# Layer 3 of a graph attention network: totals from pairs of blocks added on DVE, and a row of R anew for each chunk

## The chip, the cores and the metric

The kernel runs on one core of one Trainium2 chip. The metric is the device time of one execution in microseconds. Before the change it is 2934.87 us, the median of three runs (2932.88 to 2935.89). The engines of the core are TensorE (PE), VectorE (DVE), ScalarE (ACT), GpSimd (POOL) and SyncE (SP); each works through its own queue of instructions in order, and they wait for each other by semaphores.

## What is computed

Sixteen graphs of 1024 nodes with 256 features go through four attention layers, each with layer norm and ReLU ahead of it and a residual sum behind it. Layer 3, which the change touches, has four heads of 64 features:

```python
h = einsum('bnd,hde->bhne', nodes_embed, W)          # 4 heads of 64
for t in range(n_types):
    weight += (node_adj == t + 1) * (e_src[:, :, t, :, None] + e_dst[:, :, t, None, :])
weight = where(node_adj == 0, NEG, leaky_relu(weight, 0.01))
dst = einsum('bhij,bhje->bhie', softmax(weight), h) + bias
out = relu(dst) + h
out = (out - mean(out)) / sqrt(var(out) + EPS) * ln_gamma + ln_beta     # by head
x = x + out
```

The adjacency holds 0 and 1 only, so one edge type counts. The kernel writes the exponential of a leaky sum as a product of factors of the two nodes times the larger of two terms. One term is a row over all targets (R), the other a column of the source block. A softmax is then a sum of values times weights, divided by the sum of weights (the totals).

## The kernel before

The 16 batches go in two streams, even and odd ones. Each stream is a Python generator that yields an estimate of time; a loop takes the next piece of the stream that is behind, and the second stream starts `LAG` = 111 units late. So one stream's layer 3 lies beside the other stream's layers 0 to 2. The framework's scheduler then orders the instructions of each queue, within what the waits and `keep_in_program_order` allow.

A layer of attention (layers 0 to 2, `attend`) makes one row of R (`weigh`, a PSUM tile of two banks of which there is only one), eight weight tiles of 128 x 1024 from it on DVE (L367), and then eight accumulators of eight matmuls each (L461), of which two are in PSUM per stream. Each accumulator is evicted over DVE (L385, L386), ScalarE (L393, L395) and DVE (L396, L397), or on DVE alone in layer 0 (L501). Then the next layer's projection follows by pairs of blocks (`project`: L302 on DVE, transposes L338, ScalarE's copy L340, matmuls L345, evictions L413 and L417).

Layer 3 does for each of four heads: a row of R (the first by transposes, L374; the others from thirds of the factors in bf16, L574), eight weight tiles on DVE (L367), 64-wide values (`add_values`) and totals (`add_totals`) on TensorE. Both use tiles of 32 columns, four matmuls side by side (`in_tiles`, L586). The totals use the factor q of each source (column E of V3) as the stationary side, for each of eight blocks and two halves: 16 matmuls a head, beside 32 for the values. `acc` and `total` are both held in PSUM until the head's end, ScalarE copies them (L663), transposes turn them (L670, L678), DVE divides (L681) into `y`, and `center` and `rescale` normalise on DVE, ACT and POOL into `y`, which is then written to HBM (L704). A head's weight tiles are made while the head before is in its products, eight at a time, from one row of R; all of it comes in steps of four source blocks (`for first in range(0, NI, 4)`), here called chunks.

Of the kernel before, what the change touches and what calls it, by code (L numbers as in the profile page):

```python
# [32 lines left out]
F32 = mybir.dt.float32  # L33
BF = mybir.dt.bfloat16
# [7 lines left out]
P = 128  # L42
# [19 lines left out]
def short_path(ctx: ExitStack, tc: tile.TileContext, ins: dict, out: bass.AP, bad: bass.AP):  # L62
# [8 lines left out]
    NH = N // HALF  # L71
    NG = HALF // P
    EXT = [3, 3, 3, 3 * H]
    LAG = 111.0
    QUAD = P // 4
    ROOT_D = D**0.5
    ROOT_E = E**0.5
# [273 lines left out]

    row_taken = []

    def weigh(b: int, turn, c, op, into: list):

        while row_taken:
            yield 0.25
        row_taken.append(b)  # L360
        r = psum.tile([P, N], F32, name="row", bufs=1)
        for i in range(NI):
            turn(r[:, ts(i, P)], i)
        yield 0.5
        for j in range(NI):
            w = edges.tile([P, N], F32, name=f"weights{b % 2}")
            nc.vector.scalar_tensor_tensor(w, r, c(j), masks[b][:, j // 2, :, j % 2], op0=op, op1=ALU.mult)  # L367
            into.append(w)
            if j == NI - 1:
                row_taken.pop()  # L370
            yield 0.5

# [28 lines left out]
    def batch(b: int):  # L401
# [130 lines left out]


        h3, ex = last["h3"], last["ex"]
        y = single.tile([P, NI, H, E], F32, name="y")
        normed = []

        def center(h: int, blocks=slice(0, NI), engine=nc.gpsimd):
# [27 lines left out]
        def weigh3(h: int):  # L566
            if h == H:
                return iter(())
# [7 lines left out]
            return weigh(  # L576
                b, from_thirds if h > 0 else along_row(lambda i: ex[:, i, 2 * H : 2 * H + 1]),
                lambda j: ex[:, j, H + h : H + h + 1], ALU.max, weights,
            )

        def in_tiles(parts, accT: bass.AP, first: bool, last: bool):
# [11 lines left out]
        def halves_of(h: int, j: int):  # L593
            return [weights[h * NI + j][:, ts(g, HALF)] for g in range(NH)]
# [19 lines left out]
        behind = weigh3(0)  # L614
        yield from start(behind, b)
# [8 lines left out]
        for h in range(H):  # L624


            acc = accumulator(b)
            total = accumulator(b)
            if h == 0:
                for first in range(0, NI, 4):  # L630
                    for _ in range(4):
                        next(behind)
                    pinned = []
                    for j in (first + 2, first):
                        add_values(h, j)
                    yield 3.6
                for _ in behind:
                    pass
                turned_thirds = psum.tile([3 * QUAD, P], BF, name="misc")
                made = nc.tensor.transpose(  # L640
                    turned_thirds, thirds.rearrange("p t i h -> p (t i h)"), ident_bf
                )
                tc.keep_in_program_order(made)
                thirds_T = small.tile([3 * QUAD, P], BF, name="thirds_T", bufs=1)
                nc.scalar.copy(thirds_T, turned_thirds)
            behind = weigh3(h + 1)
            yield from start(behind, b)

            for first in range(0, NI, 4):
                pinned = []  # L650
                for j in (first + 2, first):
                    add_totals(h, j)
                    if h > 0:
                        add_values(h, j)
                for _ in range(4):
                    next(behind, None)
                yield 1.8 if h == 0 else 5.4
            for _ in behind:
                pass
            copies = []  # L660
            for accT in (acc, total) if h == 0 else (total, acc):
                copies.append(wide.tile([P, HALF], F32, name="sums"))
                nc.scalar.copy(copies[-1], accT)  # L663
                next(testing)
                next(coming, None)
            sums, totals = copies if h == 0 else copies[::-1]
# [20 lines left out]
            if h > 0:  # L687
                rescale(*normed.pop())


            if b < B - 1:
                normed.append(center(h))
            elif h < H - 1:
                normed.append(center(h, engine=nc.gpsimd if h < H - 2 else nc.vector))
            else:
                normed += [center(h, slice(g * NG, g * NG + NG), nc.vector) for g in range(NH)]
            yield 1.0
        for _ in coming:
# [406 lines left out]
```

## Time and profile before

| | us | share of the span |
|---|---|---|
| median of the runs | 2934.87 | |
| the profiled execution | 2933.13 | |
| its span, first to last instruction | 2931.4 | |
| attention matmuls (L461), TensorE busy | 1435.6 | 49% |
| values and totals of layer 3 (L586) | 691.7 | 24% |
| weight tiles of layer 3 (L367 from `ex`), DVE busy | 629.0 | 21% |
| weight tiles of layers 0 to 2 (L367 from `V`) | 473.7 | 16% |
| rows of R from thirds (L574), TensorE busy | 29.7 | 1% |

An fp32 matmul appears as two records. Records of matmuls overlap, so a group's busy time is more than what it adds to the end; the spacing from start to start tells the latter. The lines of the trace read `start, length, engine, line, operation, out<-in, count`, with the idle time ahead of the group in brackets and what ended it. A row of stages reads `stretch, length`, then the busy times of PE, weight load, DVE, ACT and POOL with their counts, the granted TensorE clock, the DMA share and GB/s.

### The profile page before, as it was taken

To read this page: it belongs to the slowest core of one execution; us is meant where nothing else is said; L and a number is where in the kernel's file an instruction comes from. 1 tells how busy PE (TensorE), PEld (TensorE's weight loads), DVE (VectorE), ACT (ScalarE), POOL (GpSimd) and SP (SyncE) were. 2 spreads that over 40 slices of the span, in tenths; PEclk is the share of its full clock that TensorE was granted. 3 is DMA by queue.
4 is the path that set the end of the run, shared out by engine and by line. 5 is a ranking of instruction groups with operands and counts; after the bars stand their busy time and mean duration, and the time that the engine had idled before them with its cause. 6 is when DMAs were issued, how large, how long until landed. Compare 5 with 4: busy or idle time off the path is not lost.

```text
span 2931.4 us, 44756 instructions
## 1 busy us (share of the span) xinstructions
PE 2810.0 (96%) x16790; PEld 1961.9 (67%) x16790; DVE 2147.9 (73%) x4490; ACT 1088.2 (37%) x3010; POOL 981.3 (33%) x1533
## 2 busy tenths in 40 slices
PE   7999999999999999999999999999999999999986
PEld 5775857668576685766758577685766857667552
DVE  5658688586976859778586885868768587685857
ACT  1333434343343433424334343433434334343332
POOL 2123324243242423424233242432424224242333
PEclk9999999999999999999999999999999999999998
DMA  8204022030321303122031220303203031110101
GB/s 126 39 8 65 30 30 58 8 51 29 37 51 16 56 17 51 37 29 59 1 51 37 30 58 8 51 30 37 51 12 47 29 49 39 15 30 1 22 22 31
DMA packets 127967, 106.14 MB, mean 36 GB/s; under 512 B 79872, under 2 KB 98432, under 8 KB 127744
## 3 DMA queue, kind: packets, MB, share of 16 engines
q0 software_dynamic: 47328, 66.10, 15.4%
q1 hardware_dynamic: 79568, 35.53, 5.4%
q8 instruction: 135, 2.21, 0.3%
q10 hardware_dynamic: 848, 1.57, 0.2%
q14 instruction: 88, 0.72, 0.1%
HBM read 153.49 MB, written 33.55 MB: 64 GB/s over the span
## 4 chain that ended last, share of the span: by engine, by line
PE 59%; DVE 26%; issue 8%; POOL 3%; ACT 3%; DMA 0%; POOLq 0%; ACTq 0%; SPq 0%; DVEq 0%
PE acc L461 36%; DVE weights L367 16%; PE acc L586 10%; PE acc L345 9%; PE misc L338 2%; DVE centered L302 2%; POOL rstd L293 2%; DVE V L417 1%; PE row L374 1%; POOL y L544 1%; DVE y L545 1%; DVE var L555 1%; ACT square L309 1%; DVE y L551 1%; DVE mean L549 1%
## 5 line engine op out<-in xcount | busy, mean ns | idle before, releaser
L461 PE MATMUL acc<-V,weights 128*128 128x257 f32 x6144 | 1435.6, 384 | 33.5 <-DVE weights L367 15.7
L461 PEld LDWEIGHTS acc<-V,weights 128*128 128x128 f32 x6144 | 1136.6, 190 | 281.9 <-DVE weights L367 75.3
L586 PE MATMUL acc<-weights,V 128*32 128x512 f32 x6144 | 691.7, 596 | 12.0 <-DVE weights L367 8.1
L367 DVE SCALAR_TENSOR_TENSOR weights<-row,ex,mask 128x1024 f32<-128x1024 f32 x512 | 629.0, 1272 | 97.3 <-PE row L574 65.8
L345 PE MATMUL acc<-W,hT 128*128 128x259 f32 (+1 forms) x2048 | 516.1, 389 | 38.1 <-ACT hT L340 26.9
L367 DVE SCALAR_TENSOR_TENSOR weights<-row,V,mask 128x1024 f32<-128x1024 f32 x384 | 473.7, 1273 | 0.8 <-PE row L374 0.8
L345 PEld LDWEIGHTS acc<-W,hT 128*128 128x128 f32 x2048 | 378.7, 190 | 135.1 <-ACT hT L340 44.4
L586 PEld LDWEIGHTS acc<-weights,V 128*32 128x32 f32 x6144 | 189.1, 110 | 417.7 <-issue 410.3
L393 ACT ACTIVATE below<-acc,inv 128x256 f32<-128x256 f32 x256 | 121.1, 473 | 813.1 <-DVE inv L386 569.6
L293 POOL TENSOR_TENSOR rstd<-rstd,minus_half 128x2 f32<-128x2 f32 (+1 forms) x321 | 292.8, 912 | 20.3
L309 ACT ACTIVATE square<-x_b,minus_mean 128x256 bf16<-128x256 f32 x504 | 255.7, 507 | 110.3 <-DVE minus_mean L332 105.3
L441 POOL TENSOR_TENSOR x_b<-x_b,beta 128x256 f32<-128x256 f32 x128 | 93.5, 731 | 488.6 <-ACT square L309 483.5
L292 POOL TENSOR_SCALAR rstd<-squared 128x2 f32<-128x2 f32 x252 | 80.0, 317 | 464.0 <-ACT square L309 451.0
L385 DVE TENSOR_SCALAR inv<-acc 128x1 f32<-128x1 f32 x256 | 39.1, 153 | 255.3 <-PE acc L461 254.0
L302 DVE TENSOR_SCALAR centered<-x_b,minus_mean 128x256 f32<-128x256 f32 x504 | 195.7, 416 | 5.1
L340 ACT ACTIVATE hT<-misc 128x512 f32<-128x512 f32 x256 | 150.2, 592 | 129.6 <-PE misc L338 129.3
L396 DVE SCALAR_TENSOR_TENSOR x_b<-below,x_b 128x256 f32<-128x256 f32 x256 | 131.8, 515 | 84.9 <-ACT below L393 83.0
L663 ACT COPY sums<-acc 128x512 f32<-128x512 f32 x128 | 74.9, 585 | 308.6 <-PE acc L586 301.0
L413 ACT ACTIVATE V<-acc,rstd 128x3 f32<-128x3 f32 x384 | 98.4, 261 | 231.1 <-PE acc L345 230.6
L417 DVE TENSOR_SCALAR V<-acc,rstd,V 128x256 f32<-128x256 f32 x256 | 131.4, 537 | 59.8 <-ACT V L413 58.9
L338 PE MATMUL misc<-ident,centered 128*128 128x128 f32 x1024 | 158.7, 277 | 13.7 <-DVE centered L325 11.5
L170 POOL DMA_DIRECT2D adj_i<-in_adj_dram x128 | 74.4, 582 | 290.1 <-ACT adj_i L175 248.8
(96 smaller groups left out, 2212.8 us busy)
## 6 DMA issues: line engine op xcount, KB each, us to landing
adj_i<-in_adj_dram POOLq DMA_DIRECT2D x128, 256.0 KB, 3.9
x_b<-in_x_dram SPq DMA_DIRECT2D x15, 1024.0 KB, 6.4
narrow<-in_adj_dram POOLq DMA_DIRECT2D x60, 256.0 KB, 9.3
out_dram<-y POOLq DMA_DIRECT2D x30, 512.0 KB, 7.5
x_b<-in_x_dram ACTq DMA_DIRECT2D x4, 256.0 KB, 6.1
narrow_half<-in_adj_dram POOLq DMA_DIRECT2D x4, 256.0 KB, 16.9
mask<-narrow SPq DMA_TRANSPOSE x60, 3.7
weights<-in_L_gnn_a_dram SPq DMA_DIRECT2D x3, 256.0 KB, 5.5
```

The source lines that it names most:

```text
L293: nc.gpsimd.tensor_tensor(r, r, minus_half.to_broadcast([P, n]), op=ALU.pow)
L302: nc.vector.tensor_scalar(centered[:, n, :], xb[:, 2 * pair + n, :], minus_mean[:, n : n + 1], 0.0, op0=ALU.add, op1=ALU.max,)
L309: nc.scalar.activation(square, xb[:, 2 * pair + n, :], AF.Square, bias=minus_mean[:, n : n + 1], accum_out=squared[:, n : n + 1],)
L338: nc.tensor.transpose(turned[:, k, ts(n, P)], centered[:, n, ts(k, P)], ident)
L340: nc.scalar.mul(hT, turned, ROOT_D)
L345: nc.tensor.matmul(projected, hT[:, k, ts(n, P)], W[l][:, k, :], start=(k == 0), stop=(k == NK - 1),)
L367: nc.vector.scalar_tensor_tensor(w, r, c(j), masks[b][:, j // 2, :, j % 2], op0=op, op1=ALU.mult)
L393: nc.scalar.activation(below, acc[:, :D], AF.Exp, scale=inv)
L396: nc.vector.scalar_tensor_tensor(xi, below, 1.0, xi, op0=ALU.min, op1=ALU.add)
L417: nc.vector.tensor_scalar(V[:, i, :D], projected[:, :D], rstd, V[:, i, D : D + 1], op0=ALU.mult, op1=ALU.mult,)
L461: nc.tensor.matmul(accs[i], weights[j][:, ts(i, P)], V[:, j, : D + 1], start=(j == 0), stop=(j == NI - 1),)
L586: made = nc.tensor.matmul(accT[ts(n, QUAD), :], values, moving, start=first, stop=last)
```

## The change

- The totals are no longer taken from the eight weight tiles. `add_up` adds two source blocks on DVE, the first times a ratio of the two blocks' q, in one `scalar_tensor_tensor`; the totals then need half of the matmuls. The sums go to two buffers `added`. The ratio is made once a batch by a reciprocal and a product.
- A row of R is made for each chunk of four source blocks of heads 2 to 4 (`weigh` with `blocks`), so the one PSUM tile is held for four weight tiles instead of eight. The first head's row still serves eight.
- The work of a head is spread: each chunk now yields more steps to the other stream, a head's totals are added one chunk later, and its `close` (copy, transposes, division, normalisation) runs inside the next head's first chunk. `total` is a PSUM tile taken at the second chunk. `LAG` is 112.
- `y` is no buffer of its own any more but the value part of V3; the last addition of `rescale` writes into `xb`, and the output is written from there.

```diff
-    LAG = 111.0
+    LAG = 112.0
...
-    def weigh(b: int, turn, c, op, into: list):
+    def weigh(b: int, turn, c, op, into: list, blocks=range(NI)):
...
-        for j in range(NI):
+        for j in blocks:
...
-            if j == NI - 1:
+            if j == blocks[-1]:
...
-        y = single.tile([P, NI, H, E], F32, name="y")
+        y = V3[:, :, :, :E]
...
-            engine.tensor_add(yh, yh, xb[:, blocks, head])
+            engine.tensor_add(xb[:, blocks, head], yh, xb[:, blocks, head])
...
-        def add_totals(h: int, j: int):
+        added, totals_of = {}, {}
+
+        def add_totals(h: int, first: int):
             parts = [
-                (V3[:, j + n, h, E:].to_broadcast([P, QUAD]), halves_of(h, j + n)[g])
-                for g, n in ((0, 1), (0, 0), (1, 1), (1, 0))
+                (
+                    V3[:, first + 2 * n + 1, h, E:].to_broadcast([P, QUAD]),
+                    added[h, first, n][:, ts(g, HALF)],
+                )
+                for g in range(NH)
+                for n in range(2)
             ]
-            in_tiles(parts, total, j == 2, j == NI - 4)
+            in_tiles(parts, totals_of[h], first == 0, first > 0)
+
+        def add_up(h: int, first: int):
+            for n in range(2):
+                s = added[h, first, n] = single.tile([P, N], F32, name="added", bufs=2)
+                j = first + 2 * n
+                w, w1 = weights[h * NI + j], weights[h * NI + j + 1]
+                nc.vector.scalar_tensor_tensor(
+                    s, w, ratio[:, j + 1, h : h + 1], w1, op0=ALU.mult, op1=ALU.add
+                )
...
+        behind = weigh3(0)
+        yield from start(behind, b)
+        for _ in behind:
+            yield 0.5
+        ratio = ex[:, :, :H]
+        nc.vector.reciprocal(ratio, ratio)
+        nc.gpsimd.tensor_mul(ratio[:, 1:], ratio[:, 1:], V3[:, : NI - 1, :, E])
+        closing = iter(())
+        to_add = []
+        for h in range(H):
+            acc = accumulator(b)
+            for first in range(0, NI, 4):
+                pinned = []
+                for j in (first + 2, first):
+                    add_values(h, j)
+                if first > 0:
+                    totals_of[h] = accumulator(b)
+                if to_add:
+                    add_totals(*to_add.pop())
+                if first == 0 and h > 0:
+                    closing = close(*to_close)
+                add_up(h, first)
+                to_add.append((h, first))
+                yield 2.5
+                if h == 0 and first == 0:
...
+                if h < H - 1:
+                    yield from weigh3(h + 1, range(first, first + 4))
+                yield 2.0
+                yield from closing
+                closing = iter(())
+                yield 2.0
+            sums = copy_of(acc)
+            to_close = h, sums
+        pinned = []
+        add_totals(*to_add.pop())
+        yield from close(*to_close)
...
-                y[:, ts(g, NG)].rearrange("p (c t) h e -> p c t (h e)", t=2),
+                xb[:, ts(g, NG), :].rearrange("p (c t) f -> p c t f", t=2),
```

More of the change, by code (lines that the diff above doesn't have):

```diff
@@ L561, in rescale, with weigh3 @@
             engine.tensor_mul(yh, yh, gamma[:, head].unsqueeze(1).to_broadcast(shape))
-            engine.tensor_add(yh, yh, xb[:, blocks, head])
+            engine.tensor_add(xb[:, blocks, head], yh, xb[:, blocks, head])
         weights = []
-        def weigh3(h: int):
-            if h == H:
-                return iter(())
+        def weigh3(h: int, blocks=range(NI)):
             def from_thirds(r: bass.AP, i: int):
@@ L577, in weigh3 @@
                 b, from_thirds if h > 0 else along_row(lambda i: ex[:, i, 2 * H : 2 * H + 1]),
-                lambda j: ex[:, j, H + h : H + h + 1], ALU.max, weights,
+                lambda j: ex[:, j, H + h : H + h + 1], ALU.max, weights, blocks,
             )
@@ L604, in add_values @@
                 in_tiles(parts, acc, n == 3, n == NI - 4)
-        def add_totals(h: int, j: int):
+        added, totals_of = {}, {}
+        def add_totals(h: int, first: int):
             parts = [
-                (V3[:, j + n, h, E:].to_broadcast([P, QUAD]), halves_of(h, j + n)[g])
-                for g, n in ((0, 1), (0, 0), (1, 1), (1, 0))
-            ]
-            in_tiles(parts, total, j == 2, j == NI - 4)
-        behind = weigh3(0)
-        yield from start(behind, b)
+                (
[4 more added lines that the diff above has]
+                for n in range(2)
+            ]
+            in_tiles(parts, totals_of[h], first == 0, first > 0)
[7 more added lines that the diff above has]
+                )
         rest = small.tile([P, NI, H], F32, name="rest", bufs=1)
@@ L623, in batch, with copy_of, close @@
         nc.gpsimd.tensor_sub(thirds[:, 2], rest, thirds[:, 1])
[L624 to L666, printed above, removed]
+        def copy_of(accT: bass.AP) -> bass.AP:
+            copied = wide.tile([P, HALF], F32, name="sums")
+            nc.scalar.copy(copied, accT)
+            next(testing)
+            next(coming, None)
+            return copied
+        def close(h: int, sums: bass.AP):
+            totals = copy_of(totals_of.pop(h))
             yield 0.5
@@ L686, in batch @@
             yield 0.5
-            if h > 0:
+            if normed:
                 rescale(*normed.pop())
@@ L695, in batch @@
             else:
-                normed += [center(h, slice(g * NG, g * NG + NG), nc.vector) for g in range(NH)]
+                normed.extend(
+                    center(h, slice(g * NG, g * NG + NG), nc.vector) for g in range(NH)
+                )
             yield 1.0
+        behind = weigh3(0)
[23 more added lines that the diff above has]
+                if h == 0 and first == 0:
+                    turned_thirds = psum.tile([3 * QUAD, P], BF, name="misc")
+                    made = nc.tensor.transpose(
+                        turned_thirds, thirds.rearrange("p t i h -> p (t i h)"), ident_bf
+                    )
+                    tc.keep_in_program_order(made)
+                    thirds_T = small.tile([3 * QUAD, P], BF, name="thirds_T", bufs=1)
+                    nc.scalar.copy(thirds_T, turned_thirds)
+                if h < H - 1:
[9 more added lines that the diff above has]
+        yield from close(*to_close)
         for _ in coming:
```

## The prediction

> **What bounds the kernel now.** I read the page's busy shares, its chain and its costliest groups first. TensorE is busy 96% of the span and leads the chain; DVE has 27% to spare.
>
> ```profile
> PE 2810.0 (96%) x16790; PEld 1961.9 (67%) x16790; DVE 2147.9 (73%) x4490; ACT 1088.2 (37%) x3010; POOL 981.3 (33%) x1533
> ...
> PE 59%; DVE 26%; issue 8%; POOL 3%; ACT 3%; DMA 0%; POOLq 0%; ACTq 0%; SPq 0%; DVEq 0%
> ...
> L586 PE MATMUL acc<-weights,V 128*32 128x512 f32 x6144 | 691.7, 596 | 12.0 <-DVE weights L367 8.1
> ```
>
> Then I cut one batch period out of the middle: from one first row of R (L374 from `ex`) at 1446.75 to the next at 1625.24, 178.5 us, with a cut wherever TensorE writes a row of R. The columns are stretch, length, then busy time of PE, weight load and DVE.
>
> ```profile
> 1446.75:1462.82 16.07, 15.81 (x119) 8.31 (x117) 11.75 (x17) 3.11 (x10) 3.35 (x10) 1.00 0.01 2
> 1462.82:1473.78 10.96, 10.96 (x97) 5.07 (x93) 10.30 (x10) 4.35 (x9) 1.17 (x2) 1.00 0.32 49
> 1473.78:1488.63 14.85, 14.15 (x93) 8.13 (x90) 14.25 (x21) 4.01 (x7) 5.99 (x8) 1.00 0.26 37
> 1488.63:1503.08 14.45, 13.95 (x97) 8.81 (x96) 14.17 (x29) 4.00 (x12) 4.56 (x6) 1.00 0.78 73
> 1503.08:1543.28 40.20, 40.02 (x275) 24.72 (x273) 30.55 (x70) 19.47 (x50) 15.94 (x18) 1.00 0.31 53
> 1543.28:1568.87 25.59, 23.30 (x114) 18.78 (x113) 22.77 (x46) 13.17 (x44) 14.06 (x18) 1.00 0.25 83
> 1568.87:1625.24 56.37, 56.31 (x273) 48.67 (x272) 29.15 (x88) 20.05 (x60) 16.38 (x35) 1.00 0.00 1
> ```
>
> The average hides two regimes. Where heads of layer 3 run (lines 2 to 4), DVE is busy 94 to 98%; in the last line it is half idle. Matmuls overlap in the records, so I price them by the spacing of starts in TensorE's timeline: 16 of L461 in 3.47 us, 48 of L586 in 5.29, 16 of L345 in 3.56, four transposes in 0.44. The period's work is then 169.7 us, and 8.8 are lost, most of it (3.7) in line 6, where projections wait for each other's evictions; lines 2 to 5 lose 0.4, 1.75, 0.85 and 1.2.
>
> At the start of layer 3, TensorE has other work while DVE makes the first four weight tiles:
>
> ```profile
> 1446.75 1.04 PE L374 MATMUL row<-ident,ex 128*128 128x128 f32 x8
> 1447.62 0.60 PE L338 MATMUL misc<-ident,centered 128*128 128x128 f32 x4
> 1448.06 3.63 PE L461 MATMUL acc<-V,weights 128*128 128x257 f32 x16
> 1451.53 1.04 PE L345 MATMUL acc<-W,hT 128*128 128x259 f32 x4
> 1452.83 3.64 PE L586 MATMUL acc<-weights,V 128*32 128x512 f32 x32 [0.26 <-DVE inverses L385]
> ```
>
> ```profile
> 1447.82 4.86 DVE L367 SCALAR_TENSOR_TENSOR weights<-row,ex,mask 128x1024 f32<-128x1024 f32 x4 [1.79 <-PE row L374]
> ```
>
> The fillers take 4.9 us, the four tiles 4.86: the wait is 0.26 us. What happens without such cover is seen at the end, where the last batch is alone:
>
> ```profile
> 2853.03 9.89 PE L586 MATMUL acc<-weights,V 128*32 128x512 f32 x64 [5.04 <-DVE weights L367]
> ```
>
> ```profile
> 2853.00:2855.00 2.00, 1.97 (x12) 0.50 0.00 0
> ```
>
> 5.04 us of waiting, and after it a granted clock of 0.50.
>
> [...] L396 (two SBUF inputs) has a median of 424 ns, but 1.51 us at 1521.34, beside a POOL operation from 1521.31 to 1522.58. [...] L545 with 512 keeps 0.60 us of spacing[...].
>
> **The change, part by part.** Sums are against this execution's 2931.4 us; the runs' median of 2934.9 lies 3.5 higher.
>
> Removed: each head's totals take 8 instructions in place of 16. An fp32 one is two records, so 8 x 2 x 4 heads x 16 batches = 1,024 records; 48 follow each other in 5.29 us, 110 ns each: -112.9 us of TensorE. Totals alone (16 at 1463.81, followed at 1465.67) cost the same.
>
> Added on TensorE: heads 2 to 4 write R twice. 3 x 8 x 16 = 384 records, eight in 0.45 us: +21.5. Net -91.
>
> Added on DVE: `add_up`, 4 per head, 256 operations on two SBUF tiles. [...] from above 1.27 (the recorded L367); I take 1.16: +297 us, and DVE goes from 73% to some 84%. [...] POOL is busy 33%, DMA issues aside about 0.29; that times a residual of 0.45 us is 0.13 each, 33 us. [...] half reaches TensorE: +16 (0 to 33).
>
> Moved: I cut the built order of both kernels at the rows of R and put the same spacings on it (on DVE: weights 1.19, 512 elements 0.62, evictions 0.33 to 0.48). Before, each batch repeats the seven lines above. After, two unlike batches make a period, because layer 3 now reaches over more of the other stream: 327.4 us of TensorE against 339.4 for two batches before, and 302 of DVE against 256. DVE's slack is nearly all in one stretch (63 of TensorE, 30 of DVE); in the other 264 us of TensorE, DVE has 272. So the engines are level there, and each wait between them counts.
>
> *Even batches from the third on, start of layer 3.* Behind the row from `ex` only four projection instructions (1.8 us) are left as filler: the 16 attention records have gone elsewhere. Walked by hand from the end of that row (0): DVE makes three weight tiles, two evictions (L417) and the fourth tile by 5.7; TensorE, idle since 1.8, waits 4.0 for it. The first values end at 9.3. The next transposes wait 1.5 for `centered`, which stands on DVE behind tiles five to eight (10.5). The other values and the totals end at 15.7. DVE has made two sums by 13.4, but the next two need the two `added` buffers, which these totals free: so they start at 15.7, and with two evictions and the four tiles of head 2, which stand behind them, DVE is at 23.9. TensorE is ready at 18.5 for the other stream's row of R; that needs the one PSUM tile of rows, which those four tiles read: 5.4 us of waiting. Behind that row in TensorE's queue stand head 2's values and the other stream's attention. With 0.6 for the copy of thirds_T the stretch loses 11.5, against 0.7 before.
>
> The first even batch still has fillers; for the other seven that is 7 x 10.8 = +76. Waits of 4 and 5 us can halve the clock, as above. There, L586's first 24 records at 0.50 took 4 us in place of 2.6, about 1.5 too much: seven times +10 (0 to 20).
>
> *The later heads.* Here a head's weights are made two chunks ahead, and the walk finds slack: 2.2 us of waiting in an even batch, where before lost 3.8 in lines 3 to 5. In an odd one it finds 5.7, of which 2.0 is an accumulator of the other stream: its reciprocal stands behind a sum on DVE, ScalarE's eviction behind that, and the next attention product waits for the bank. Over two batches 7.9 against 7.6: nothing. The loss of line 6 I leave as it is.
>
> *The tail.* Alone, the last layer 3 is DVE's: 16 more sums are 18.6, of which DVE's 7.9 idle us at 2857.6 takes a part: +10.
>
> At nothing: `y` in V3, the final add into `xb` and the output from `xb` (same shapes and queues; a slot of `xb` is needed again only a batch later), 16 reciprocals and 16 POOL products (under 0.5 us, beside the weights). The order of POOL and SP keeps its DMAs.
>
> Sum: -91 + 76 + 10 + 16 + 10 = +21, so 2956 in the runs' median.
>
> **The rivals.** *TensorE stays the bound (the other side: faster).* One mechanism: DVE finds, in the stretch where it is half idle, enough lead that the first tiles and sums of an even batch come in time. Then only the records count: -91 + 10 for the tail, 2854; with half of the 11.5 us left, 2895. For it: in lines 2 to 4 DVE was as full, and only 3 us were lost. Against it: every wait there had filler, and DVE can't begin before the row of R, which TensorE writes last. It decides when that stretch loses under 6 us.
>
> *The sums reach TensorE everywhere.* Each of 256 stands in DVE's queue ahead of some eviction or weight tile; the walk lets them hide but for the places named. If a third of their 297 us shows, that is +99 in place of nothing[...]; if a fifth, 3015. For it: 264 us of level load, and the odd batch's 2.0 us is such a wait. Against it: in lines 2 to 4 DVE had 40.6 us of work by spacing and they took 40.3, so it runs close to its sum.
>
> *The change doesn't do what it says*: the built order excludes it, with 2,560 value and totals matmuls for 3,072 and 768 rows from the thirds for 384.
>
> **Chances.** The forecast's case (2925 to 2990) 0.50; sums everywhere (2990 up) 0.25; TensorE as bound (below 2925) 0.20, and 0.05 for an effect I have not seen, on either side. About 0.2%, 6 us, is what a measurement of this kernel can tell from no change. The forecast's case puts 0.07 within that and 0.43 above; slower is then 0.43 + 0.25 + 0.02 = 0.70, same 0.07, faster 0.23. The likeliest case's own range is 2925 to 2990. The range for 8 in 10, 2885 to 3025, reaches half-way into both rivals[...].
>
> **What would show it.** The line of L586 with 5,120 records and some 580 us; 768 records of the thirds' rows; 256 sums on DVE of about 1.2 us, some of them over 2 where POOL reads; DVE busy near 2450 us. In an even batch's start of layer 3: a wait of TensorE near 4 us on DVE's weights, one near 5 ahead of the other stream's row, and a clock under 1 behind them. The last layer 3 longer by about 10 us. I am wrong towards 2854 if those two waits are under 1 us, and towards 3025 if waits of attention products on ScalarE's evictions, 11.5 us in the whole trace of before, grow to several times that in every head.

## The result, and the profile after

The kernel after takes 3094.04 us in the median of four runs (3092.38 to 3094.66), the kernel before 2933.88 beside it: a ratio of 1.0544, with a 95% interval of 1.0526 to 1.0562. The prediction was 2956 us, with 2885 to 3025 as the range for 8 in 10. The kernel became slower, as forecast, but by 160 us and not by 21.

The page of the kernel after: busy shares, the chain that ended last, and two of the costliest groups.

```profile
PE 2803.8 (91%) x16150; PEld 1979.1 (64%) x16150; DVE 2457.2 (79%) x4762; ACT 1088.1 (35%) x3010; POOL 1059.5 (34%) x1549
...
PE 45%; DVE 38%; issue 7%; POOL 5%; ACT 3%; DMA 1%; POOLq 0%; ACTq 0%; DVEq 0%; SPq 0%
...
L585 PE MATMUL acc<-weights,V 128*32 128x512 f32 x4096 | 503.8, 636 | 42.2 <-DVE weights L367 42.2
...
L625 DVE SCALAR_TENSOR_TENSOR added<-weights,ex,weights 128x1024 f32<-128x1024 f32 x256 | 331.3, 1314 | 26.7 <-PE acc L585 25.9
```

TensorE lost records (16,790 before) but hardly any busy time (2810.0 before), and its share fell from 96% to 91%. Much of the busy time is slow: the mean granted clock fell from 0.995 to 0.966. The stretches with a clock of 0.50 come to 213 us, in which TensorE is busy for 151; in the kernel before they come to 28 us with 9. Half of this busy time is an estimate of what the slow clock cost (eight transposes took 1.94 us at 0.50, 1.04 at 1.00): 76 us, and 5 before. DVE's part of the chain rose from 26% to 38%. DVE is busy for 79% only, so no engine is full all the time: the rest is lost where two engines wait for each other.

First the place that the prediction named, the start of layer 3 in an even batch, in TensorE's timeline (start, length, instruction, and in brackets the idle time ahead of it):

```profile
1332.94 1.92 PE L345 MATMUL acc<-W,hT 128*128 128x259 f32 x8
1339.16 5.34 PE L585 MATMUL acc<-weights,V 128*32 128x512 f32 x32 [4.30 <-DVE weights L367]
...
1358.09 1.94 PE L374 MATMUL row<-ident,V 128*128 128x128 f32 x8 [5.52 <-DVE weights L367]
1359.96 5.57 PE L585 MATMUL acc<-weights,V 128*32 128x512 f32 x32
```

The two waits are there, 4.30 and 5.52 us (4.0 and 5.4 forecast). What follows them is longer than forecast: 32 values take 5.3 to 5.6 us where they take 3.6 elsewhere, and the eight transposes 1.9 in place of 1.0. The granted clock was 0.50 from 1341 to 1343 us, with 0.75 and 0.90 in the two microseconds before and behind, and again 0.50 from 1358 to 1362.

Then a place that the prediction left as it was, the hand-over from attention to projection at the end of layer 3:

```profile
1455.75 0.44 PE L338 MATMUL misc<-ident,centered 128*128 128x128 f32 x2 [1.16 <-DVE inv L654]
1457.15 1.17 PE L345 MATMUL acc<-W,hT 128*128 128x268 f32 x4 [0.96 <-ACT above L395]
1458.15 0.38 PE L338 MATMUL misc<-ident,centered 128*128 128x128 f32 x2
1461.09 0.66 PE L338 MATMUL misc<-ident,centered 128*128 128x128 f32 x2 [2.55 <-DVE centered L302]
1461.55 3.66 PE L345 MATMUL acc<-W,hT 128*128 128x259 f32 x8
```

Three waits in some 6 us, and behind them eight projection records in 3.66 us at a clock of 0.50, where eight took 1.92 at 1332.94. DVE's timeline for these microseconds shows why `centered` is late:

```profile
1456.08 0.98 DVE L385 TENSOR_SCALAR inv<-inv 128x8 f32<-128x8 f32 x1
...
1457.57 0.91 DVE L396 SCALAR_TENSOR_TENSOR x_b<-below,x_b 128x256 f32<-128x256 f32 x1
...
1458.59 0.42 DVE L397 SCALAR_TENSOR_TENSOR x_b<-above,x_b 128x256 f32<-128x256 f32 x1
...
1458.94 0.69 DVE L663 TENSOR_TENSOR V<-misc,inv 128x512 f32<-128x512 f32 x1
...
1459.75 1.46 DVE L302 TENSOR_SCALAR centered<-x_b,minus_mean 128x256 f32<-128x256 f32 x2
```

Around the additions of the other stream (L396, L397) stands the closing of a head of layer 3 (L385 on 8 elements, L663). Three of the instructions are stretched, each beside a POOL operation of layer 3's normalisation: L385 took 0.98 us (its median is 0.17) beside one from 1455.74 to 1457.03, an addition 0.91 in place of 0.42 beside one from 1457.11 to 1458.20, and the two `centered` 1.46 (0.60 for two at 1343.70) beside one from 1459.70 to 1460.79. That is some 2.2 us in all, nearly the length of the wait. No sum stands here; what is late is a chain of short instructions. Such encounters were there before, too: over the whole trace these kinds (L302, L385, L396, L397 and L332) lie 104 us above their medians, and 80 us in the kernel before, so that by themselves they can't make up the 160 us.

Periods tell more than single places do. From the first row of R (L374 from `ex`) of one even batch to that of the next, the mean of five, the kernel before needs 357.0 us, the one after 375.7. TensorE's work in it, by the prediction's spacings, is 339.4 and 327.4 us, so 17.6 us are lost before and 48.3 after. What the slow clock costs is part of the loss.

### The profile page after: what moved, and what is told of

Its sections match the earlier page's. It is cut to its first block, busy times and chain, and to the rows that moved or that the text cites. A ratio compares the mean times of both kernels' runs of the same rounds, so it can differ in the third digit from the quotient of the medians.

```text
span 3092.6 us, 43763 instructions
## 1 busy us (share of the span) xinstructions
PE 2803.8 (91%) x16150; PEld 1979.1 (64%) x16150; DVE 2457.2 (79%) x4762; ACT 1088.1 (35%) x3010; POOL 1059.5 (34%) x1549
## 4 chain that ended last, share of the span: by engine, by line
PE 45%; DVE 38%; issue 7%; POOL 5%; ACT 3%; DMA 1%; POOLq 0%; ACTq 0%; DVEq 0%; SPq 0%
PE acc L461 26%; DVE weights L367 17%; PE acc L345 8%; PE acc L585 7%; DVE added L625 4%; DVE x_b L397 2%; POOL rstd L293 2%; PE misc L338 2%; DVE centered L302 2%; DVE x_b L396 2%; ACT square L309 1%; DVE V L417 1%; POOL rstd L292 1%; DVE var L556 1%; PE row L374 1%
## 5 line engine op out<-in xcount | busy, mean ns | idle before, releaser
L461 PE MATMUL acc<-V,weights 128*128 128x257 f32 x6144 | 1433.5, 385 | 56.7 <-ACT above L395 33.1
L461 PEld LDWEIGHTS acc<-V,weights 128*128 128x128 f32 x6144 | 1150.7, 192 | 289.4 <-ACT above L395 45.3
L367 DVE SCALAR_TENSOR_TENSOR weights<-row,ex,mask 128x1024 f32<-128x1024 f32 x512 | 631.6, 1275 | 13.5 <-PE row L573 8.4
L345 PE MATMUL acc<-W,hT 128*128 128x259 f32 (+1 forms) x2048 | 541.4, 399 | 37.0 <-ACT above L395 26.4
L585 PE MATMUL acc<-weights,V 128*32 128x512 f32 x4096 | 503.8, 636 | 42.2 <-DVE weights L367 42.2
L367 DVE SCALAR_TENSOR_TENSOR weights<-row,V,mask 128x1024 f32<-128x1024 f32 x384 | 470.1, 1276 | 14.9 <-PE row L374 14.9
L625 DVE SCALAR_TENSOR_TENSOR added<-weights,ex,weights 128x1024 f32<-128x1024 f32 x256 | 331.3, 1314 | 26.7 <-PE acc L585 25.9
L585 PEld LDWEIGHTS acc<-weights,V 128*32 128x32 f32 x4096 | 128.6, 116 | 332.3 <-issue 318.7
L293 POOL TENSOR_TENSOR rstd<-rstd,minus_half 128x2 f32<-128x2 f32 (+1 forms) x321 | 330.5, 1030 | 21.1
L302 DVE TENSOR_SCALAR centered<-x_b,minus_mean 128x256 f32<-128x256 f32 x504 | 204.5, 436 | 4.6 <-PE misc L338 1.3
L338 PEld LDWEIGHTS misc<-ident,centered 128*128 128x128 f32 x1024 | 122.3, 143 | 75.8 <-issue 27.0
L545 POOL TENSOR_TENSOR V<-V,bias 128x512 f32<-128x512 f32 x62 | 89.8, 1449 | 209.4 <-DVE V L663 143.7
```

The costliest lines, as they stand in the source:

```text
L293: nc.gpsimd.tensor_tensor(r, r, minus_half.to_broadcast([P, n]), op=ALU.pow)
L302: nc.vector.tensor_scalar(centered[:, n, :], xb[:, 2 * pair + n, :], minus_mean[:, n : n + 1], 0.0, op0=ALU.add, op1=ALU.max,)
L338: nc.tensor.transpose(turned[:, k, ts(n, P)], centered[:, n, ts(k, P)], ident)
L345: nc.tensor.matmul(projected, hT[:, k, ts(n, P)], W[l][:, k, :], start=(k == 0), stop=(k == NK - 1),)
L461: nc.tensor.matmul(accs[i], weights[j][:, ts(i, P)], V[:, j, : D + 1], start=(j == 0), stop=(j == NI - 1),)
L585: made = nc.tensor.matmul(accT[ts(n, QUAD), :], values, moving, start=first, stop=last)
```

## The experiments

The theories, as the expectations number them: 1, the start of layer 3 lacks other work, and the waits there are the cause; 2, the sums load DVE, wherever the streams stand; 3, the rows anew and their hand-overs; 4, the closing of a head inside the next one; 5, formed after the eighth run, how the two streams mesh, that is, which of their stages stand beside each other.

Differences in this table are between medians, each to the runs of the kernel before made beside it (2933.0 to 2935.5 us). "Lost" is the period less TensorE's work in it; the work is 339.4 or 327.4, with 14.1 more where the totals stay on TensorE in the kernel after and 14.1 less where the kernel before takes them from sums (1,024 records of 110 ns in eight periods), and 2.7 more for rows anew in the kernel before.

| kernel | LAG | us | to before | period | lost |
|---|---|---|---|---|---|
| before | 111 | 2933.9 | | 357.0 | 17.6 |
| before, LAG 108 | 108 | 2942.3 | +8.4 | 357.1 | 17.7 |
| before, y in V3 | 111 | 2931.6 | -2.5 | 356.7 | 17.3 |
| before, y in V3, LAG 112 | 112 | 3036.3 | +102.1 | 370.0 | 30.6 |
| before, LAG 118 | 118 | 3032.8 | +99.0 | 367.6 | 28.2 |
| before, rows anew | 111 | 2957.8 | +24.7 | 359.9 | 17.8 |
| before, sums on DVE | 111 | 3264.6 | +330.4 | 399.4 | 74.1 |
| after | 112 | 3094.0 | +160.2 | 375.7 | 48.3 |
| after | 115 | 3154.2 | +220.0 | 384.1 | 56.7 |
| after | 118 | 3112.3 | +176.8 | 377.2 | 49.8 |
| after, no sums | 112 / 115 / 118 | 2978.3 / 2963.1 / 2988.0 | +42.8 / +28.9 / +53.8 | 362.0 / 358.9 / 361.4 | 34.6 / 31.5 / 34.0 |
| after, totals on TensorE | 112 / 115 / 118 | 3100.1 / 3010.7 / 3036.6 | +164.6 / +76.5 / +102.4 | 378.8 / 365.5 / 368.6 | 37.3 / 24.0 / 27.1 |

**The start of layer 3, by another LAG.** Theory 1 took the two waits at the start for the cause.

```diff
-    LAG = 112.0
+    LAG = 118.0
```

> The kernel after with LAG 118 for 112, nothing else. In the built order TensorE then has 5.2 to 5.3 us of work between the first row of R and the first values and 5.3 to 6.2 us before the next row, in every batch; with 112 it alternates between 1.8 / 10.2 (even batches) and 4.9 / 3.5 (odd ones). Theory 1 (the start of layer 3 lacks work of the other stream, and TensorE waits for VectorE's weights there and runs at half clock behind the wait): the 16.7 us that the starts lose per two batches go, seven times over, so about 110 us less than the kernel after, 2970 to 3000 us. Theory 2 (VectorE has too much to do with the 256 sums, wherever the streams stand): the waits move elsewhere, 3070 to 3100 us.

Measured: 3112.32 us, ratio 1.0609 (1.0592 to 1.0627). The waits of TensorE (total, times, longest), of the kernel after:

```profile
PE row L374 <- DVE weights L367: 54.3, 23, 5.5
PE acc L585 <- DVE weights L367: 42.2, 17, 5.0
...
PE misc L338 <- DVE centered L302: 21.2, 16, 2.6
...
PE acc L461 <- DVE weights L367: 7.6, 9, 1.4
```

and with LAG 118:

```profile
PE misc L338 <- DVE centered L302: 47.7, 35, 2.4
PE acc L461 <- DVE weights L367: 41.1, 67, 1.5
...
PE acc L585 <- DVE weights L367: 17.6, 9, 5.0
...
PE row L374 <- DVE weights L367: 6.1, 7, 0.9
```

That is outside both ranges, and the time rose. The start is cured: 54.3 and 42.2 us of waiting became 6.1 and 17.6, 73 us less. But the waits for `centered` and for the other stream's own weights grew by 60 us together, and some others a little. The mean granted clock even rose, from 0.966 to 0.979. Theory 1 falls as the cause of the time: that wait is where the lateness shows, and it can show elsewhere.

**The sums left out, and the totals back on TensorE.** Two runs take back opposite parts of the change. In the first, the totals read a constant, which leaves out the denominators of the softmax:

```diff
-                s = added[h, first, n] = single.tile([P, N], F32, name="added", bufs=2)
...
-                nc.vector.scalar_tensor_tensor(
-                    s, w, ratio[:, j + 1, h : h + 1], w1, op0=ALU.mult, op1=ALU.add
-                )
+                added[h, first, n] = fixed
```

> The kernel after without its 256 sums on VectorE: the totals' matmuls read a constant tile instead, so the softmax denominators are left out (the totals are wrong), while TensorE's instructions and the schedule stay. VectorE has 331 us less to do. Theory 1 (schedule): the wait at the start of layer 3 is for eight weights that have no sums among them, so it stays; only the ends and the heads gain: 3000 to 3040 us. Theory 2 (VectorE's load): the time falls by most of the 160 us above before and by TensorE's 91 us too: 2850 to 2900 us.

In the second, `add_totals` is that of the kernel before, called ahead of each `add_values`; `total` is taken together with `acc` at the head's start, and both are copied at its end:

```diff
                 for j in (first + 2, first):
+                    add_totals(h, j)
                     add_values(h, j)
...
-                add_up(h, first)
-                to_add.append((h, first))
```

> The kernel after with the totals as before: each source block's weights go through TensorE by themselves (1,024 matmuls more, 113 us), no sums on VectorE (331 us less), and the spread over the heads and the row for each chunk kept. Theory 2 (VectorE's load is what costs): below the kernel after, 2960 to 3010 us. Theory 1 (the start of layer 3, which keeps its 1.8 us of work in even batches): TensorE's 113 us come back, ends and heads give 90 back: 3090 to 3150 us.

Measured: 2978.31 us without sums (ratio 1.0148, 1.0131 to 1.0165) and 3100.13 us with the totals on TensorE (1.0561, 1.0543 to 1.0579). From the second to the first, 1,024 fewer records save 121.8 us; the two also differ in how long `total` is held in PSUM and in a chunk's delay of the totals, so not all of it need be the records. From the first to the kernel after, the sums on DVE cost 117.3. So the exchange that gives the change its name comes out even at this LAG. What is left is 164.6 us for the spread schedule, its LAG and the rows without any sum. The second run lies in theory 1's range, the first outside both. In the kernel with the totals on TensorE, too, the start keeps its waits:

```profile
PE row L374 <- DVE weights L367: 58.4, 23, 5.0
PE acc L585 <- DVE weights L367: 36.8, 10, 5.0
```

And without the sums the second wait of an even batch's start is 5.05 us, with sums 5.52 (TensorE's line, then DVE's):

```profile
1315.28 1.94 PE L374 MATMUL row<-ident,V 128*128 128x128 f32 x8 [5.05 <-DVE weights L367]
```

```profile
1310.27 4.86 DVE L367 SCALAR_TENSOR_TENSOR weights<-row,ex,mask 128x1024 f32<-128x1024 f32 x4 [0.27 <-PE row L573]
```

DVE waits here for head 2's row and then makes the four tiles, and the other stream's row stands behind them. So that wait belongs to the hand-over of the one PSUM tile of rows. The sums ahead of the tiles add only 0.5 us to it.

**One row of R a head.** The generator of `weigh3(h + 1)` is taken once and stepped four weights at a time.

```diff
-                    yield from weigh3(h + 1, range(first, first + 4))
+                    if first == 0:
+                        behind = weigh3(h + 1)
+                        yield from start(behind, b)
...
```

> The kernel after with one row of R for each head (taken at the first chunk and held to the second), instead of a row for each chunk; 8 matmuls of a row a head less, 21.5 us of TensorE in all. Theory 3 (the rows anew, and their hand-overs between the streams, cost more than their matmuls): 3020 to 3060 us. Theories 1 and 2: what TensorE gains (about 20 us) and no more, 3065 to 3085 us; the row is held longer, so a loss of up to 20 us (3115 us) would show that the change's second row pays for itself.

Measured: 3143.55 us (1.0713, 1.0695 to 1.0731), 48 us more than the kernel after, outside both. In the spread schedule the second row pays. The likely reason, that a row held over two chunks keeps the other stream from its own row, was not tested by itself.

**Both suspects away.** LAG 118, once without the sums and once with the totals on TensorE:

> The kernel after without its 256 sums (constant tile for the totals, denominators left out, as before in the run without sums) and with LAG 118: both suspects away at once, TensorE's instructions those of the kernel after. So far LAG 118 alone gave +18 us and no sums alone -116 us. If the two add up (theory 1 and 2 both hold, and with the sums away VectorE is free enough for the work between row and values to be enough): the starts' 13 to 17 us per two batches go, 2860 to 2890 us. If LAG only moves VectorE's lateness from one place to another whatever its load: 2970 to 3000 us.

> Totals on TensorE as before, no sums on VectorE, LAG 118: the spread schedule and the row for each chunk alone, with work of 5.2 us between row and values in every batch. If the spread is harmless once the start has work: 2931 + 21 for the rows' matmuls, and some waits, 2955 to 2990 us. If the spread itself (closing a head inside the next one, values and weights further apart) makes the other stream late: 3070 to 3110 us, near the 3100 us with LAG 112.

Measured: 2987.97 us (1.0186, 1.0169 to 1.0203) and 3036.57 us (1.0349, 1.0332 to 1.0367). Without sums LAG 118 gains nothing, so the cured start is worth nothing there either. With totals on TensorE it gains 62 us, between the two ranges and without reaching the kernel before. The sums cost 123.0 us at this LAG.

**The sums in the old schedule.** The kernel before with `add_up` after each chunk's values, and the totals of the pair sums one chunk later.

```diff
-                for j in (first + 2, first):
-                    add_totals(h, j)
-                    if h > 0:
+                if h > 0:
+                    for j in (first + 2, first):
                         add_values(h, j)
+                    if first > 0:
+                        add_totals(h, 0)
+                    add_up(h, first)
...
```

> The kernel before, its schedule, one row of R a head and LAG 111 kept, with only the totals changed: 256 sums by pairs on VectorE and 1,024 matmuls of them instead of 2,048 (y in V3 and the output from xb, to make room). TensorE 113 us less, VectorE 331 us more. Rival A (the sums cost only in the spread schedule): 2830 to 2870 us. Theory 2 (VectorE's load costs wherever it lands): 2950 to 3010 us; from the pair of runs with and without sums in the spread schedule (116 us) the sum 2931 - 113 + 116 gives 2934 us.

Measured: 3264.58 us (1.1123, 1.1105 to 1.1142). Its waits:

```profile
PE acc L586 <- DVE added L626: 134.4, 88, 5.3
PE acc L586 <- DVE weights L367: 63.1, 47, 5.7
```

That is far above both ranges. Rival A falls. In the kernel after, TensorE waits for the sums themselves for 8.9 us in all; here for 134.4. So the sums need some such spread: it hides the wait for them, and costs something of its own.

**The small parts, and LAG in the kernel before.** Five runs. First y in V3, the output from `xb` and LAG 112 together, then without the LAG, then LAG 108 and 118 alone:

> The kernel before with three small parts of the change alone: y in V3, the output from xb, LAG 112 for 111. In the built order LAG 112 leaves TensorE 2.2 us (4.8 before) of work between the first row of R and the first values in odd batches, and 5.2 in even ones. Theory 1: such a start loses some 2 to 3 us with its half clock, seven times, 2945 to 2960 us. If y and LAG do nothing: 2930 to 2940 us.

> The kernel before with y in V3 and the output written from xb, LAG 111 kept: the small parts of the change without the shift of LAG, which together gave +102 us. If LAG 112 was the cause (the two streams then mesh differently from batch to batch): 2930 to 2940 us. If y in V3 is the cause (V3 is held until the last head is normalised, xb until the output has left, so the next batch starts later): 3020 to 3040 us.

> The kernel before with LAG 108 for 111, nothing else. In the built order the first batch starts otherwise, then both streams mesh as with 111: 4.8 and 9.9 us of TensorE's work around the first row in every batch. Theory 5 in its narrow form (not the size of LAG but the mesh that it leads to sets the time): 2930 to 2950 us. If any shift of LAG costs, as 112 did (+102 us): 2980 to 3040 us.

> The kernel before with LAG 118, nothing else. In the built order two patterns alternate, 5.8 / 8.8 and 4.8 / 9.9 us, so no start has less work between row and values than with LAG 111 (LAG 112 had starts of 2.2 us). Theory 1 in the kernel before (the short starts were what LAG 112 cost): 2930 to 2950 us. Theory 5 (the alternation itself, that is, which stages of the two streams stand beside each other): 2980 to 3040 us.

Measured: 3036.25 us (1.034, 1.0322 to 1.0359); 2931.64 us (0.9992, 0.9985 to 0.9999); 2942.25 us (1.0027, 1.0016 to 1.0038); 3032.79 us (1.0335, 1.0318 to 1.0353). So y in V3 costs nothing. One unit of LAG, from 111 to 112, costs the old kernel over 100 us, outside both ranges, and three units the other way 8, which is lost by the second batch's first row (385.9 us in place of 375.7). Not the number matters but the mesh that the streams settle into. With LAG 118 no start of layer 3 is short of other work, and it is as slow as with 112. TensorE's timeline of that run has the first rows of three batches at

```profile
1312.03 1.04 PE L374 MATMUL row<-ident,ex 128*128 128x128 f32 x8
...
1521.83 1.04 PE L374 MATMUL row<-ident,ex 128*128 128x128 f32 x8
...
1678.94 1.04 PE L374 MATMUL row<-ident,ex 128*128 128x128 f32 x8
```

which is 209.8 and 157.1 us apart. The kernel before has 178.5 and 178.5 with LAG 111 and with 108, and about 195 and 175 with 112. The kernel after has 167 and 208:

```profile
1332.07 1.04 PE L374 MATMUL row<-ident,ex 128*128 128x128 f32 x8
...
1499.18 0.27 PE L374 MATMUL row<-ident,ex 128*128 128x128 f32 x1
...
1707.21 1.04 PE L374 MATMUL row<-ident,ex 128*128 128x128 f32 x8
```

**LAG 115**, whose built order gives every batch of the kernel after the same start:

> The kernel after with LAG 115 for 112. In the built order both streams then mesh alike in every batch (5.3 us of TensorE's work before the values and 5.3 after, each time), as they do in the kernel before with LAG 111 (4.8 and 9.9 each time); with 112 and 118 two patterns alternate. Theory 5 (a new one: the alternating mesh is what costs, in the kernel before too, where LAG 112 alternates 2.2 and 5.2 and was 102 us slower): 2980 to 3030 us. Theory 2 alone (VectorE's sums): 3085 to 3115 us, as with 112 and 118.

> Totals on TensorE as before, no sums on VectorE, the spread and the rows anew kept, LAG 115, with which both streams mesh alike (5.2 and 5.3 us in every batch). Theory 5: the loss of 165 us (LAG 112) and 102 us (LAG 118) against the kernel before shrinks to the rows' matmuls and some waits, 2950 to 2985 us. If the spread itself makes the ends of the other stream's layers late: 3030 to 3100 us.

> No sums (constant tile for the totals, denominators left out) and LAG 115, both streams meshing alike. Theory 5: 2860 to 2900 us, that is 100 us or so below the same kernel with LAG 112 (2978) and 118 (2988). If the mesh is nothing: 2975 to 2990 us. Against the kernel after with LAG 115 it gives the price of the sums on VectorE, 116 us with LAG 112 and 124 us with LAG 118.

Measured: 3154.22 us (1.0751, 1.0733 to 1.0769), 3010.67 us (1.0259, 1.0242 to 1.0276) and 2963.12 us (1.0098, 1.0081 to 1.0115). With the totals on TensorE it is the best mesh of three, 88 us better than LAG 112, though above what theory 5 expected and below the other range. Without sums it gains 14 us of the 100 expected. With the sums it is the worst of three, so theory 5 falls for the kernel after, and evenness is no rule: there the first rows are some 183 and 201 us apart, more even than with LAG 112. The sums cost 191.1 us in this mesh.

**How the sums cost.** The same 256 sums in 512 pieces with a turn of the other stream after each, and sums of half the columns:

```diff
-                nc.vector.scalar_tensor_tensor(
-                    s, w, ratio[:, j + 1, h : h + 1], w1, op0=ALU.mult, op1=ALU.add
-                )
+                for g in range(NH):
+                    nc.vector.scalar_tensor_tensor(
+                        s[:, ts(g, HALF)], w[:, ts(g, HALF)], ratio[:, j + 1, h : h + 1],
+                        w1[:, ts(g, HALF)], op0=ALU.mult, op1=ALU.add,
+                    )
+                    yield 0.5
```

> The kernel after, LAG 112, its 256 sums on VectorE cut into 512 of half the columns, each with a turn of the other stream behind it (the same turns as before in all), so that the other stream's short instructions on VectorE wait for 0.65 us at a time instead of two sums in a row, 2.5 us. If the sums cost because they stand in VectorE's queue ahead of short instructions that TensorE waits for: half to two thirds of the 116 us that the sums cost at LAG 112 come back, 3010 to 3050 us. If it is the time that VectorE needs, in whatever pieces: 3085 to 3110 us (512 instructions have some overhead).

> The kernel after, LAG 112, with sums of the first 512 columns only (1,024 elements before), which the totals of the other 512 columns read as well; the denominators of half the rows are left out. VectorE has some 160 us less to do, all the rest is as after. If the cost goes with VectorE's time: half of 116 us comes back, 3025 to 3045 us. If it has a threshold (only what exceeds a slack costs): either nearly all or nearly nothing comes back, 2980 to 3000 or 3075 to 3095 us.

Measured: 3110.65 us (1.0606, 1.0589 to 1.0624) and 3023.93 us (1.0309, 1.0292 to 1.0326). Pieces don't help: they cost 17 us, with DVE's time for the sums up from 331 to 371 us. That speaks against the block of two sums in the queue as the cause, though the pieces also take more of DVE's time. Half the columns do help. The group in that run:

```profile
L625 DVE SCALAR_TENSOR_TENSOR added<-weights,ex,weights 128x512 f32<-128x512 f32 x256 | 198.3, 800 | 36.3 <-PE acc L585 35.5 <-POOL ex L691 0.4
```

133 us less of DVE gave 69 us of the end, over half of the 117; the remaining 198 us cost 48. So in this mesh the cost goes with DVE's time, steeper at the top by these two steps, without a slack that hides the sums whole.

**Rows alone.** The kernel before with `weigh3(h + 1, range(4))` ahead of the first chunk and `range(4, 8)` ahead of the second.

> The kernel before, LAG 111, with one part of the change: a row of R anew for each chunk of four weights in heads 1 to 3, so 384 matmuls of a row more, 21.5 us of TensorE by their own spacing. The mesh of the streams in the built order stays (4.8 and 9.9 us in every batch). If a row costs its matmuls: 2950 to 2965 us. If the hand-over costs (TensorE's next row stands behind the four weights of the row before, which VectorE has yet to make): 2975 to 3020 us. If it helps (the row is free for the other stream sooner): below 2945 us.

Measured: 2957.75 us (1.0083, 1.0066 to 1.01), and 178.5 us between first rows became 179.9: the mesh held. In the old schedule a row costs little more than its matmuls, and the hand-over that was feared is in the waits with 2.1 us in all.

**Closing at the head's end**, with totals on TensorE and LAG 115:

```diff
-                    closing = close(*to_close)
...
-            to_close = h, sums, totals
-        yield from close(*to_close)
+            yield from close(h, sums, totals)
```

> The kernel with totals on TensorE, LAG 115 (3010.7 us), with one part of the spread undone: a head is closed at its own end, as before, not inside the first chunk of the next head. If the closing inside the next head is what makes the ends late: 2960 to 2990 us. If it is the right place and the loss lies in the mesh and the rows: 3015 to 3060 us.

Measured: 3057.37 us (1.042, 1.0404 to 1.0437), 48 us above the same kernel with the closing inside the next head. It moves where the yields stand, so it changes the mesh too; what it shows is that closing a head at its own end doesn't win the time back.

No version here beats the kernel before by more than can be told: y in V3 alone is 2.5 us faster, below the 0.2% that the prediction set for that.

## Why the prediction was wrong

At LAG 112 the difference of 160.2 us splits along the runs, in the order before, rows, spread, fewer totals, sums: +24.7, +139.9, -121.8, +117.3. The spread includes LAG 112 here. The split depends on the order and on the mesh: at LAG 115 it would be +24.7, +51.8, -47.6, +191.1.

- **TensorE's records: their number right, their worth only at one LAG.** -112.9 forecast, -121.8 measured here. But at LAG 115 and 118 the same records bring only 48 and 49 us, so the agreement at LAG 112 is in part luck: in two meshes of three, less than half of what was taken from TensorE came off the end.
- **The rows: right** in the old schedule, +21.5 forecast, +24.7 measured; in the spread one they save 48. **y in V3: right**, at nothing.
- **The price of a sum: right.** 297 us of DVE forecast; the records add up to 331, but they overlap. DVE's next instruction starts 1.196 us behind a sum's start, 306 us in all, and DVE's busy time rose by 309. The 1.16 us a sum in the forecast was the author's estimate; the kernel before has no such sum. **The sums beside POOL: too high.** Nine sums of 256 took over 2 us (2.19 to 2.30), each beside POOL operations of layer 3's normalisation, and all lie 9 us above their median in total, where 33 were forecast. That a sum beside a POOL operation waits for it was the author's estimate, and most didn't: 111 ran beside one (DMA issues aside), with the median of all, 1.278 us. Neither was the failing step.
- **The start of layer 3: places and lengths of the waits right, one reason wrong, the clock short.** The second wait was put down to sums that delay the tiles; the run without sums has 5.05 of its 5.52 us, so that its length came out was partly luck. By the spacings it loses 18.1 us in two batches, 1.4 before: seven times 16.7 is 117, against the forecast's 76 and 10. The term "about 1.5 too much" for the half clock came out at 4.6 in each even batch (half of TensorE's busy time at 0.50), since the clock was 0.50 behind the second wait as well. Over the whole trace the slow clock costs some 71 us more than before, where +10 (0 to 20) stood: it also fell at the ends of layer 3 and in the tail. Much of this lies inside the losses given here, so it isn't added to them.
- **"The loss of line 6 I leave as it is": this step failed.** The hand-overs at the ends of layer 3 lose 19.5 us in two batches in place of 9.8 (lines 5 and 6 of the prediction's table), seven times 9.7 or 68 us, where the sum had nothing. The later heads, also "nothing", lose 3.5 more, 25 us in seven. The tail, from the last transpose of the last batch's first row to the end, is 102.2 us and was 83.7: +18.5, forecast +10. With the -91 of the records, these places come to 138 of the 160 us; the other 22 are not placed.
- **The assumption under that step.** The forecast priced each place by itself and carried the rest over. The run with LAG 118 shows that places are not independent: the dearest one was cured and the sum stayed. The forecast had written "the engines are level there, and each wait between them counts"; taken seriously, that meant DVE's 297 us had to be charged as a whole, not where a walk met them. Rival 2 did that: "If a third of their 297 us shows". 117 of 306 us is 38%, and 191 at LAG 115 is 62%. Put in place of the places, it would still have missed the mesh. The sign that was named for this side did come, since the waits of attention products on ScalarE's evictions grew from 11.5 to 33.1 us; but they are 33.8 us without any sum, so it was not the sums that made them.
- **The mesh was not a term at all.** LAG 112 for 111 was in the diff and got no price, as the new spread got none. In the kernel before that unit is worth 105 us (3036.25 to 2931.64, each to its own runs of before). How much of the spread's 139.9 us is mesh can't be told exactly; 88 of it goes with LAG 115. Which pair of stages collides in a bad mesh stays open: the runs show that it decides, and that neither the filler at the start nor even distances explain it.

## What to carry to other kernels

Where two streams are interleaved by estimates, move the offset by a unit each way in both kernels before judging an edit: here one unit alone was worth 3.5%, beside 5.4% for the whole change. Work shifted from the leading engine to one with slack "on average" is to be charged at a fraction of its length everywhere, here a third or more, unless the receiving engine is seen to idle in that very stretch. And when one wait is cured and the time stays, look at the list of waits for the one that grew.

## What the hardware showed beyond that

At the end of layer 3 the granted clock fell to 0.50 in a wait of 2.55 us, with waits of 1.16 and 0.96 us just ahead. Stretches of the kernel after (stretch, length, TensorE busy and count, granted clock, DMA share, GB/s):

```profile
1457.00:1459.00 2.00, 1.39 (x6) 1.00 0.00 0
1459.00:1461.00 2.00, 0.00 (x0) 0.62 0.00 0
1461.00:1462.00 1.00, 0.91 (x4) 0.50 0.00 0
```

The clock fell while TensorE still waited, 1.6 us before its next matmul, and stayed at 0.50 to beyond 1465. In the kernel after, from 20 us on, the clock fell in or just behind (1.1 us at most) every one of the 28 idle stretches of TensorE between 2.4 and 7 us, and behind none of the 28 between 1.0 and 1.5 us. So in this kernel waits of 2.5 us must be priced with a slow stretch behind them.

A sum of two SBUF tiles of 1,024 fp32 elements has a median of 1.278 us, and one of 512, in the run with half the columns, has 0.747: by these two, an estimate of 1.04 ns an element and 0.22 us fixed. From the start of a sum of 1,024 to that of the next instruction on DVE, where it follows at once, the median is 1.196 us: that is what a sum takes from DVE, against 1.192 for the weight tiles (L367) of the kernel before. The prediction's 1.16 lies 0.04 us below this spacing, and 0.12 below the record.
